# A scan and expert kernel whose engines' order is found by playing 2700 parts through, instead of by a table of places

## The chip, the cores and the metric

The kernel runs on one core of a Trainium2 chip. A core has several engines, each with its own queue of instructions that it works off in order: TensorE (PE in the profile; its weight loads are shown as PEld), VectorE (DVE), ScalarE (ACT), GpSimd (POOL) and SyncE (SP). SP and POOL issue the transfers between main memory and on-chip memory; POOL issues those whose rows are chosen by a list of indices. The engines run side by side and wait for each other through semaphores. Matrix products are written to PSUM, a small on-chip memory that is read by ACT and DVE.

The metric is the time on the device in microseconds (us), the median of three runs.

## The reference

The input x has 2 batches of 2048 tokens of 256 numbers, all in 32-bit floats. Each token is normalized (xn). Two branches are added to x:

```python
x = x + selective_scan_branch(xn) + moe(xn)
```

The scan branch puts each batch's tokens in the order of the cluster that they are nearest to (8 clusters, a stable sort), projects each sorted token to a step size and to two vectors B and C of 16 numbers, and then runs along the 2048 tokens, for each of 256 channels and 16 states:

```python
dA = jnp.exp(d_t[..., None] * A)
h = dA * h + (d_t * u_t)[..., None] * b_t[:, None, :]
y = jnp.einsum('bdn,bn->bd', h, c_t)
```

The result goes back to the tokens' first places. The expert branch picks for each token the two best of 8 experts and adds their outputs, weighted; an expert is `silu(x w1) * (x w3)`, 512 wide, times w2.

## The kernel before, in words

**The front** (until about 68 us) loads x, finds norms, clusters and experts, and writes the normalized rows to main memory (`xn`). It makes lists: which tokens the 71 expert tiles (128 rows each, of one expert) hold (`token_of`), which row of the weights each tile's loads start at (`w_row`), and which token stands at each place of the sorted order (`line_of`, by `list_rows`). The change does not touch the front.

**Expert tiles** (class `Tile`). Tile t goes through: `load_rows` gathers 128 rows (`xg_sb`, four buffers); `turn` transposes them on PE, copies them to `xT` on ACT and finds each row's share `own` on DVE; `up(0)` and `up(1)` are the products with w1 and w3 on PE, eight matmuls each, into one PSUM bank each; after `up(0)` comes a tanh on ACT, then `silu` on DVE, and after `up(1)` the `gate` on DVE; `down` is the product with w2 on PE, scaled on ACT (`yo`) and added to the sums in main memory (`acc`) by an indirect DMA of POOL. `load_up` and `load_down` fetch the weights for tile t + 3 into the buffers that tile t has left (1 MB and 0.5 MB). Where the expert is the same as three tiles before, the list of rows points outside and nothing is fetched. Every add into `acc` waits until the adds before it have landed (`wait_for_adds`).

**Scan pieces and steps** (classes `Piece` and `Step`). Each batch's sorted tokens are cut in four pieces of 512. A piece is gathered (`gather`, four indirect DMAs), transposed (`turn`), projected (`project`), its B and C are stored in main memory and loaded again spread over all partitions (`load_b`, `load_z`), and its step sizes are found (`step_size`, `decay_of_one`, `log`, `series`). A piece has four steps, by halves of states and of channels, which makes 32 steps. In a step ACT makes eight decays (`da`, `decay`), DVE makes four products `bu` (`feed`) and four scans over 1026 elements (`scan`), and PE turns the states (`turn`, 32 transposes into two PSUM buffers `pt_s`, copied to `ht` by ACT) and contracts them with C (`contract`, 32 matmuls into `y`). When a piece is done, `take_sums` copies its y and `add_sums` adds it to `acc` with four indirect DMAs. The last piece is added to the output itself, after `acc` has been copied there.

**What sets the order.** Each engine's queue holds its instructions in the order of the program's text; a chain of dependencies at the end of the kernel pins this. The text is written by hand. A list `lead` gives the first 13 expert jobs with the first piece's preparation between them. After that the steps are walked in eight places each: the even ones hold a scan, the odd ones a feed; places 1, 2, 4 and 5 turn the previous step's states in pairs, places 3 and 6 contract 16 matmuls at once. A table `plan`, filled by `at_place`, puts the next piece's preparation at fixed places. Expert jobs (`up(0)`, `up(1)`, and the previous tile's `down`, in this turn) are given out so that estimated PE work keeps a fixed ratio to estimated DVE work; `silu` and `gate` follow two places after their product (`later`).

## Time and profile before

| | us |
|---|---|
| median of 3 runs | 839.67 (839.21 to 841.74) |
| the profiled execution | 846.96 |
| its span, first to last instruction | 845.2 |
| PE, DVE, POOL, ACT busy | 728.7, 674.0, 577.3, 510.0 |
| first scan starts, last scan starts | 119.20, 821.65 |
| one scan, one feed on DVE | 2.297, 1.221 |
| last down-product of an expert tile ends | 801.5 |

A row of the profile names a line of the kernel, an engine, an operation, what is written and read (`out<-in`), how often, the busy time and the mean of one in ns, and the idle time before it with what ended it. In a listing in order of time the first two numbers are the start and the length in us. Matmuls of 32-bit floats show as two each. The spans on POOL are rough.

### The profile page before, as it was taken

How to read it: one execution, taken by the hardware profiler on the slowest of the kernel's cores; microseconds unless marked ns; L12 is line 12 of the kernel's file. 1: busy time of each engine (PE TensorE's matmuls, PEld its weight loads, DVE VectorE, ACT ScalarE, POOL GpSimd, SP SyncE). 2: the span in 40 equal slices, each digit the busy share in tenths (PEclk: the TensorE clock that was granted, in tenths of full speed). 3: DMA queues.
4: the chain of work that ended last, by engine and by line, in shares of the span. 5: the costliest groups of instructions: out<-in, count | busy, mean ns of one | idle time of the engine just before them, and what ended most of it. 6: DMA issues, size and time to landing. Idle time of an engine off the chain costs nothing.

```text
span 845.2 us, 16770 instructions
## 1 busy us (share of the span) xinstructions
PE 728.7 (86%) x6552; PEld 607.4 (72%) x6552; DVE 674.0 (80%) x849; ACT 510.0 (60%) x986; POOL 577.3 (68%) x374
## 2 busy tenths in 40 slices
PE   7376889789998998999989888899999898989564
PEld 5236677579987887788868776688778786979443
DVE  8964179589996989799879786788979897989590
ACT  4721265386667666866676565756695667757372
POOL 2024558677868778888868687886788888888412
PEclk9656999999999999999999999999999999999896
DMA  9683353854577548655674657556754855455472
GB/s 285 236 251 114 59 157 65 247 135 97 119 221 169 122 92 266 144 123 138 192 165 102 164 154 190 94 140 179 201 102 103 263 157 97 85 112 104 78 213 26
DMA packets 74015, 125.90 MB, mean 149 GB/s; under 512 B 24976, under 2 KB 42544, under 8 KB 70672
## 3 DMA queue, kind: packets, MB, share of 16 engines
q0 software_dynamic: 40224, 65.03, 32.7%
q1 hardware_dynamic: 33712, 59.80, 25.8%
q8 instruction: 52, 0.85, 0.4%
q14 instruction: 27, 0.22, 0.1%
HBM read 180.06 MB, written 27.00 MB: 245 GB/s over the span
## 4 chain that ended last, share of the span: by engine, by line
PE 51%; DMA 13%; ACT 11%; issue 9%; POOL 8%; DVE 7%; POOLq 0%; SPq 0%; ACTq 0%; DVEq 0%
PE p_ps L889 20%; PE py L912 10%; PE pt_s L800 7%; PE y L810 4%; POOL acc L830 4%; DMA w<-in_w_up_dram,w_row 4%; DMA w<-in_w_down_dram,w_row 4%; ACT ht L804 3%; POOL w L849 2%; ACT da L769 2%; DMA out_dram<-acc 2%; PE px L649 2%; PE pd L687 2%; PE pl L331 1%; DVE st L363 1%
## 5 line engine op out<-in xcount | busy, mean ns | idle before, releaser
L784 DVE TENSOR_TENSOR_SCAN hs<-da,bu 128x1026 f32<-128x1026 f32 x128 | 294.0, 2297 | 11.2 <-ACT da L769 1.9
L889 PE MATMUL p_ps<-xT,w 128*128 128x128 f32 x2272 | 280.2, 280 | 12.1 <-DMA w<-in_w_up_dram,w_row 5.3
L889 PEld LDWEIGHTS p_ps<-xT,w 128*128 128x128 f32 x2272 | 268.6, 195 | 29.0 <-issue 14.4
L830 POOL DMA_INDIRECT acc<-yo,token_of x71 | 141.0, 1985 | 68.8 <-ACT da L769 11.5
L769 ACT ACTIVATE da<-dl,na 128x512 f32<-128x512 f32 x256 | 181.3, 725 | 0.2 <-DVE hs L784 0.2
L912 PE MATMUL py<-w,g 128*128 128x256 f32 x568 | 145.8, 402 | 30.8 <-DMA w<-in_w_down_dram,w_row 19.2
L776 DVE TENSOR_TENSOR bu<-du,bt 128x1026 f32<-128x1026 f32 x128 | 156.3, 1221 | 19.5 <-ACT bt L756 15.7
L804 ACT COPY ht<-pt_s 128x512 f32<-128x512 f32 x256 | 137.3, 588 | 43.4 <-PE pt_s L800 36.7
L800 PE MATMUL pt_s<-ident,hs 128*128 128x128 f32 x1024 | 140.0, 280 | 20.0 <-ACT ht L804 14.6
L800 PEld LDWEIGHTS pt_s<-ident,hs 128*128 128x128 f32 x1024 | 115.7, 143 | 48.9 <-ACT ht L804 29.5
L849 POOL DMA_INDIRECT w<-in_w_up_dram,w_row x71 | 99.9, 1407 | 74.4 <-DVE w_row L578 36.2
L912 PEld LDWEIGHTS py<-w,g 128*128 128x128 f32 x568 | 107.4, 199 | 49.6 <-issue 14.2
L849 POOL DMA_INDIRECT w<-in_w_down_dram,w_row x71 | 111.7, 1573 | 21.6 <-issue 15.8
L863 POOL DMA_INDIRECT xg_sb<-xn,token_of x71 | 100.5, 1416 | 37.9 <-issue 17.4
L916 ACT ACTIVATE yo<-py,own 128x256 f32<-128x256 f32 x71 | 33.8, 476 | 103.9 <-PE py L912 99.1
L897 ACT ACTIVATE t_sb<-p_ps 128x512 f32<-128x512 f32 x71 | 42.5, 599 | 82.9 <-PE p_ps L889 71.5
L830 POOL DMA_INDIRECT acc<-yt,line_of x28 | 68.8, 2456 | 24.4 <-ACT ht L804 11.9
L902 DVE SCALAR_TENSOR_TENSOR t_sb<-t_sb,p_ps 128x512 f32<-128x512 f32 x71 | 48.5, 683 | 43.3 <-ACT t_sb L897 34.7
L810 PE MATMUL y<-ht,z 128*32 128x128 f32 x2048 | 76.8, 278 | 4.5 <-ACT ht L804 2.2
L810 PEld LDWEIGHTS y<-ht,z 128*32 128x32 f32 x2048 | 49.8, 109 | 25.3 <-ACT ht L804 11.3
L906 DVE SCALAR_TENSOR_TENSOR g<-t_sb,p_ps 128x512 f32<-128x512 f32 x71 | 48.4, 681 | 14.5 <-PE p_ps L889 8.9
L874 ACT COPY xT<-pt_g 128x256 f32<-128x256 f32 x71 | 26.8, 378 | 40.1 <-PE pt_g L872 40.0
(194 smaller groups left out, 580.0 us busy)
## 6 DMA issues: line engine op xcount, KB each, us to landing
bt<-bc SPq DMA_DIRECT2D x64, 512.0 KB
z<-bc SPq DMA_DIRECT2D x32, 256.0 KB
xn<-xt SPq DMA_DIRECT2D x8, 520.0 KB
xt<-in_x_dram SPq DMA_DIRECT2D x8, 512.0 KB
acc<-in_x_dram SPq DMA_DIRECT2D x8, 512.0 KB
w<-in_w_up_dram,w_row POOLq DMA_INDIRECT x71
w<-in_w_down_dram,w_row POOLq DMA_INDIRECT x71
xg_sb<-xn,token_of POOLq DMA_INDIRECT x71
```

The costliest lines, as they stand in the source:

```text
L769: nc.scalar.activation(self.da[o][:, n, 1:], self.piece.dl[:, self.h, :], AF.Exp, scale=na[:, self.h, state : state + 1],)
L776: nc.vector.tensor_mul(self.bu[o], self.piece.du[:, self.h, :].unsqueeze(1).to_broadcast([P, 2, CH1]), self.piece.bts[2 * self.s + o // 2] ...
L784: nc.vector.tensor_tensor_scan(self.hs.rearrange("p n t o -> p (n t) o")[:, :, o], self.da[o].rearrange("p n t -> p (n t)"), self.bu[o].re ...
L800: nc.tensor.transpose(pt[:, j, :], self.hs[:, n, t0 : t0 + G, :].rearrange("p t o -> p (t o)"), ident)
L804: nc.scalar.copy(self.ht[i], pt)
L810: nc.tensor.matmul(p.ys[self.h][j * G : (j + 1) * G, i, :], lhsT=p.zs[q][:, i * (P // G) + j, :], rhs=self.ht[i][:, j, :], start=False, st ...
L830: ins = nc.gpsimd.indirect_dma_start(out=to, out_offset=bass.IndirectOffsetOnAxis(ap=numbers, axis=0), in_=rows, in_offset=None, compute_o ...
L849: nc.gpsimd.indirect_dma_start(out=to[self.t % NW], out_offset=None, in_=rows, in_offset=bass.IndirectOffsetOnAxis(ap=w_row[:, self.t : se ...
L863: nc.gpsimd.indirect_dma_start(out=self.xg, out_offset=None, in_=xn_d, in_offset=bass.IndirectOffsetOnAxis(ap=token_of[:, self.t : self.t ...
L889: nc.tensor.matmul(p[:, f, :], lhsT=wk[:, h, f * P : (f + 1) * P], rhs=self.xT[:, h, :], start=h == 0, stop=h == ND - 1,)
L902: nc.vector.scalar_tensor_tensor(self.s, self.s, 1.0, self.p1, ALU.add, ALU.mult)
L912: nc.tensor.matmul(py, lhsT=self.g[:, f, :], rhs=w2[:, f, :], start=f == 0, stop=f == NH - 1)
```

## The change

The counts of scans, feeds, decays, matmuls and DMAs stay the same; what changes is where the order comes from. All steps above are cut into some 2700 parts, each on one engine: what was one method with a product, its copy by ACT and an add by POOL is now three (`turn`, `take_turned`, `find_own`; `up`, `tanh`; `down`, `take_down`, `add`). `contract` handles four matmuls at a time. The list of a batch's sorted rows (`list_rows`) becomes a class `RowList` with parts of its own, and its product with `part_p` moves from ACT to DVE.

A part has an engine, a cost in us, a due time, the parts that it needs, a time that its data take to land, and buffers that it takes until other parts have ended. `play` goes through the parts on paper: an engine that is free begins, among the parts that are able and whose buffers are free, the one with the smallest due time. The order in which parts begin is the order in which they are written to the text. The front, the tiles' buffers and the chain of dependencies at the end stay.

```diff
-    def list_rows(b: int, pos):
+    class RowList:
...
+            nc.vector.tensor_scalar(
+                self.num[:, 0], self.num[:, 2], part_p[:, self.b : self.b + 1], None, ALU.mult
+            )
...
-        def contract(self, n: int):
+        def contract(self, n: int, i: int):
             p, q = self.piece, 2 * self.s + n
-            for i in range(JC):
-                for j in range(P // G):
...
+            for j in range(P // G):
...
+    def play(parts, signal: float):
...
+        def able(p):
+            at = max([q.landed() + (signal if q.engine != p.engine else 0.0) for q in p.needs], default=0.0)
+            ready[p.engine].append((p.due, number[p], at, p))
...
+                r = min(able_now)
...
+                p.ended = busy[engine] = now + p.cost
+                begun.append(p)
...
+    slots = {
...
+            m=2, t=2, h0=1, h1=1, y0=1, y1=1, tok=4, member=1, xd=2, dl=2, du=2, w=1, b=2, z0=1, z1=1,
+            z2=1, z3=1, da=3, bu=2, hs=2, ht=4, yt=2, xT=2, own=6, s=2, g=2, yo=3, xg=4, add=1, lst=1,
...
+    END = 690.0
+    E0, S0 = 8.0, 45.0
+    TILE = (END - 30.0 - E0) / NT
+    STEP = (END - S0) / len(steps)
...
+        due = E0 + n * TILE
...
+            xg = Part(POOL, 1.25, due - 20.0, t.load_rows, (), 2.5)
+            wu = Part(POOL, 1.35, due - 20.0, t.load_up, [ups[n - NW]], 9.0)
+            wd = Part(POOL, 1.35, due - 18.0, t.load_down, [downs[n - NW]], 9.0)
+        turn = Part(PE, 0.3, due - 5.0, t.turn, [xg])
+        take = Part(ACT, 0.38, due - 8.0, t.take_turned, [turn])
+        own = Part(DVE, 0.4, due - 4.0, t.find_own, [xg])
+        up0 = Part(PE, 2.0, due, lambda t=t: t.up(0), [take, wu])
+        tanh = Part(ACT, 0.6, due - 8.0, t.tanh, [up0])
+        up1 = Part(PE, 2.0, due + 2.0, lambda t=t: t.up(1), [take, wu, up0])
+        silu = Part(DVE, 0.7, due - 8.0, t.silu, [tanh])
+        gate = Part(DVE, 0.7, due - 8.0, t.gate, [silu, up1])
+        down = Part(PE, 2.0, due + 4.0, t.down, [gate, wd])
+        yo = Part(ACT, 0.48, due - 2.0, t.take_down, [down, own])
+        add = Part(POOL, 1.95, due + 4.0, t.add, [yo], 2.5)
+        xg.take(slots["xg"], turn, own)
+        turn.take(slots["m"], take)
...
+                        Part(ACT, 0.73, at_o - 9.0, lambda st=st, i=i: st.decay(i), [series[2], *decay])
...
+                feed = Part(DVE, 1.25, at_o - 3.0, lambda st=st, o=o: st.feed(o), [series[3], begin_b])
+                scan = Part(DVE, 2.3, at_o, lambda st=st, o=o: st.scan(o), [feed, *decay, *step_scans[-1:]])
...
+                        PE, 0.55, at_i, lambda st=st, j=j, i=i: st.turn(j, i), [step_scans[-1], *step_turns[-1:]]
...
+                        PE, 0.15, at_i, lambda st=st, j=j, i=i: st.contract(j, i),
...
+            add = Part(POOL, 7.8, due + (SPP + 1) * STEP, lambda p=p: p.add_sums(acc_d), sums, 2.5)
...
+    for p in play(parts, 0.15):
+        p.do()
```

As built, PE's queue has each tile's `down` ahead of the next tile's second product, where before it stood behind both, and the transposes and contractions of a step stand in groups of four among the expert products. POOL's queue mostly has the down load of tile t + 3 ahead of tile t's add, where before it stood behind it. All expert tiles are through on PE before the transposes of step 30 (counted from 0), before the change ahead of those of step 29.

## The prediction

> **What bounds the kernel now.** I read the page first, then busy time by stretch, then the waits of TensorE (PE) inside the long stretch, then single rows. The page shows three engines near their limit and none at it:
>
> ```profile
> span 845.2 us, 16770 instructions
> ...
> PE 728.7 (86%) x6552; PEld 607.4 (72%) x6552; DVE 674.0 (80%) x849; ACT 510.0 (60%) x986; POOL 577.3 (68%) x374
> ```
>
> Busy time by stretch (columns: start and end, length, then PE, PEld, DVE, ACT, POOL, each with its count, granted clock, DMA share, GB/s):
>
> ```profile
> 68.00:120.00 52.00, 42.97 (x248) 34.80 (x249) 19.28 (x47) 20.13 (x34) 23.83 (x22) 0.84 0.45 126
> 120.00:790.00 670.00, 619.15 (x5813) 528.72 (x5811) 575.71 (x599) 436.30 (x853) 526.20 (x311) 0.99 0.60 145
> 790.00:801.50 11.50, 3.75 (x10) 2.96 (x11) 3.69 (x3) 0.49 (x2) 5.18 (x3) 0.70 0.28 37
> 801.50:845.00 43.50, 22.23 (x288) 15.90 (x286) 20.60 (x12) 21.88 (x42) 9.32 (x6) 0.81 0.46 116
> ```
>
> The stretches are: lead (first expert tiles until about the first scan), body, a hole, tail (no expert tiles left). In the body PE is busy 619.15 of 670 us (92%), VectorE (DVE) 86%. GpSimd (POOL) looks like 79%, but nearly every one of its 311 DMA instructions is preceded by about 0.30 us of idling, mostly put down to "issue": 526.2 + 311 x 0.30 = 619.5 us, also 92%. So PE idles only 50.9 us in the body, 9.0 in the lead and 7.75 in the hole: 67.6 us from 68 to 801.5, with 665.9 us of work. That idle time, and the tail's 43.7 us, are all that an order can win back. What PE waited for in the body (total, times, longest):
>
> ```profile
> PE py L912 <- DMA w<-in_w_down_dram,w_row: 10.8, 6, 3.8
> PE pt_s L800 <- ACT ht L804: 10.7, 14, 1.0
> PE py L912 <- ACT r L691: 6.0, 5, 2.0
> PE p_ps L889 <- DMA w<-in_w_up_dram,w_row: 5.3, 3, 2.7
> PE py L912 <- ACT u L636: 2.8, 5, 1.1
> PE p_ps L889 <- ACT xT L874: 2.7, 2, 1.5
> ...
> PE y L810 <- ACT ht L804: 2.2, 7, 0.5
> ```
>
> By kind: expert weights 16.1 us; turned states (ht) 12.9; other handovers with ScalarE (r, u, xT, yo, by all rows of that answer) 15.0; the remaining 6.9 small.
>
> **The change, part by part.** Counts of scans, feeds, matmuls and DMAs stay; the order of every queue is new from the first expert tile on.
>
> *Row lists.* For each of two lists the products by part_p go from ACT (0.396 us, L325) to DVE. No such DVE row exists; the nearest, L326 at 0.225 us, times 4 is 0.9 us, plus two small conversions of 0.17: 1.2 us of DVE, between 0 (the body has 94 us of idle DVE) and 1.2 if that cover goes. I take 0. The second list also no longer stands as one block in which DVE waits for PE: that was one wait of 8.2 us at 150 us, while PE itself waited 3.8 us for weights, so I count no separate gain.
>
> *Lead.* On PE the first turning of states now follows 7 tiles' up-products, not 9, but on DVE five gates, not four, stand before the first scan, and the four gathers of the first piece are mixed with weight loads that wait for tiles 0 and 1. One gate is 0.68 us; one tile on PE is 2 x 1.95 + 1.85 = 5.8 us. Between -6 and +6; I take 0 and keep 9.0 us idle.
>
> *Weights.* Still three buffers, so a load still waits for the tile three before. What moves is POOL's queue: before, every down load stood behind the same tile's add, which waits for the add before to land; now most stand ahead of it. The hole is such a case:
>
> ```profile
> 792.59 2.55 POOL L830 DMA_INDIRECT acc<-yo,token_of  x1 [7.44 <-DMA acc<-yt,line_of]
> 795.45 1.07 POOL L849 DMA_INDIRECT w<-in_w_down_dram,w_row  x1 [0.30 <-issue]
> ...
> 797.75 3.71 PE L912 MATMUL py<-w,g 128*128 128x256 f32 x8 [8.38 <-DMA w<-in_w_down_dram,w_row]
> ...
> 802.70 1.23 DVE L776 TENSOR_TENSOR bu<-du,bt 128x1026 f32<-128x1026 f32 x1 [8.90 <-ACT bt L756]
> ```
>
> The add waits 7.44 us, the load behind it goes out late, PE waits 8.38 us, ACT's yo behind PE, and DVE 8.90. In the new order the last down load follows the piece's four adds directly. So the hole's 7.75 us goes to 0, and down waits from 10.8 to 5 (between 0 and 10.8); up waits keep 5.3. That makes 10.3.
>
> *Handovers.* Copies out of PSUM are now parts of their own, and a PE part is written only when a PSUM slot is free on paper: ht 12.9 to 4.5, others 15.0 to 5. Ends: 0 and all 27.9; I lean to the low end because the durations written into the parts (scan 2.3, feed 1.25, decay 0.73, up 2.0) are those of the rows (2.297, 1.221, 0.725, 1.79 to 1.98). Small ones keep 6.9.
>
> *A new tightness.* Before, a whole other tile stood on PE between a tile's second up-product and its down-product: by row prices (up 1.94, eight transposes 1.04, sixteen contractions 1.08) a median 10.7 us. Now it is 2.2 us, and for 21 of 71 tiles 1.1 to 1.7. In that time DVE must do the gate, 0.68 us, behind whatever scan it has begun, 2.30. Queued behind a waiting down-product on PE are transposes and contractions, for which ACT and then DVE wait. Lower end 0; upper (2.30 + 0.68 - 2.2) x 71 = 55 us. I take, for the 21 tight ones, half a scan plus the gate less 1.4 us of cover: 0.43 x 21 = 9.0, nearer the low end, since the order was laid with these durations.
>
> *Finer grain.* Contractions stand in 196 runs instead of 64, transposes in 216 instead of 108. Each of 132 more contraction runs may cost nothing or the 0.17 us seen before contractions in the tail: 0 to 22; I take 0, since other matmuls follow at once in the body.
>
> *POOL.* The parts give it 5.9 us a tile (1.25 + 1.35 + 1.35 + 1.95); the rows say 1.42 + 1.41 + 1.57 + 1.99 + 4 x 0.30 = 7.6. It will run behind its paper times; whether PE feels that is a rival below. Its length comes from company on DVE (first minimum, median and maximum ns; then a load begun under a scan):
>
> ```profile
> L849 POOL DMA_INDIRECT w<-in_w_down_dram,w_row x71: 993/1415/3051, 44.1 to 795.5; - x71
> ```
>
> ```profile
> 119.20 2.30 DVE L784 TENSOR_TENSOR_SCAN hs<-da,bu 128x1026 f32<-128x1026 f32 x1
> 119.38 2.93 POOL L849 DMA_INDIRECT w<-in_w_up_dram,w_row  x1 [2.31 <-PE pt_g L872]
> ```
>
> The Trainium skill, page "SBUF — State Buffer", section "Who interferes with whom", says that a DVE instruction with two SBUF inputs contends with a GpSimd instruction that reads SBUF, and that the loser of the shared ports is blocked, not slowed. That speaks against a change that packs DVE more tightly. Taken strictly, scans and feeds would shut POOL out for 294 + 156 us, and with 396 us at its shortest durations and 103 of issue it would need 949 us, more than this span; the rows above, which reach 3 us but have a median of 1.4, disagree, and the sum goes by them.
>
> *Tail.* Behind the last gate stood eight scans, now five; behind the last down-product 96 transposes and 96 contractions, now 76 and 84. Two paths lead to the last adds:
>
> ```profile
> 811.12 1.21 SPq L1141 DMA_DIRECT2D out_dram<-acc  x2
> ...
> 824.09 3.79 PE L800 MATMUL pt_s<-ident,hs 128*128 128x128 f32 x16 [4.88 <-DVE hs L784]
> ...
> 833.79 1.54 POOL L830 DMA_INDIRECT out_dram<-yt,line_of  x1 [24.93 <-ACT yt L731]
> ```
>
> Scans: last gate, 5 x 3.52 = 17.6, then 9.6 as from 823.95 to 833.5, less 3.7 until the last down-product: 23.5 us after it. Copy: 801.5 to 826.4 was 25.0 (chain of waits: 811.74 plus 14.70); up to 30 if a fourth add must land first. I take 25.0, then 11.4 for the last adds as now (833.8 to 845.2): 36.5 instead of 43.7, between 35 and 41.4. The 20 transposes and 12 contractions add 3.4 us to PE's work before that, and the last down-product, 3.71 us at clock 0.70, gives back 1.9.
>
> **Sum.** Idle: 9.0 + 10.3 + 9.5 + 6.9 + 9.0 = 44.7. Span: 68 + 665.9 + 1.5 + 44.7 + 36.5 = 816.6 (before by the same sum: 68 + 665.9 + 67.6 + 43.7 = 845.2). The profiled run took 846.96, 1.8 over its span and 7.3 over the median 839.67, so the median is 816.6 + 1.8 - 7.3 = 811.
>
> **Rivals.**
> - *The paper order holds fully.* Only the lead's 9.0 us stay idle and the tail is 35: 68 + 667.4 + 9 + 35 = 779, median 774 to 795 with some rest. For it: durations on PE, DVE and ACT match the rows. Against: POOL does not, and weights still come three tiles ahead.
> - *Lockstep (the other side).* PE and DVE wait for each other at nearly every tile because the 2.2 us of cover are less than a scan plus a gate (2.98): 55 in place of 9.0 gives a span of 863, median 857. It decides from 28.6 us more idle than my sum, 0.40 us a tile. For it: the 21 tight tiles and POOL's drift. Against: the paper has DVE free at that moment.
> - *POOL sets the pace.* Its work from 64.3: 564.5 + 344 x 0.30 less the last four adds, 660 us. With DVE denser (86 to 93%) busy time grows 8%, 45 us; if it also keeps its 51 us of body waits, then with 30.5 from landing to end the span is 851, median 845. Half of these waits: 819. Against: loads now stand ahead of adds.
> - *No use.* Idle time only changes place: 67 us of it with the shorter tail, median 833.
>
> **How the numbers follow.** Likeliest (795 to 832) 0.42; paper order 0.18; POOL or idle moved, split: 832 to 837 0.05, within 0.3% (837.2 to 842.2, about what three runs of 839.21 to 841.74 can tell) 0.04, POOL above that 0.13; lockstep 0.18. Faster 0.65, same 0.04, slower 0.31. The range is 776 to 868: below lies little of the paper case, above the worse half of lockstep with finer grain. The likeliest alone: 795 to 832.
>
> **What would show it.** Right: the 8.4 us wait of py for down weights gone; PE waits on r, u and xT below 5 us; PE idle in the body under 45 us; fewer than six scans behind the last gate; the last adds released by the copy, not by yt. Wrong: PE rows waiting on DVE g, or DVE's t_sb waiting on ACT, each well over 10 us; POOL busy plus issue above 97% with PE waiting for w or xg_sb; granted clock falling below 0.97 in the body, which would raise the price of every matmul.

## The result, and the profile after

The changed kernel takes 880.39 us (median of 4 runs, 879.78 to 885.34) against 840.70 for the kernel before on the same chip: a ratio of 1.047 (95% interval 1.042 to 1.053). It is slower. The forecast of 811 us had the wrong sign, and its range (776 to 868) does not hold the time.

The page of the kernel after, its span and its busy times:

```profile
span 878.5 us, 16650 instructions
...
PE 761.4 (87%) x6552; PEld 608.3 (69%) x6552; DVE 674.1 (77%) x853; ACT 520.1 (59%) x982; POOL 545.8 (62%) x374
```

The profiled execution took 880.27 us. The one of the kernel before took 846.96, 6.3 over the median of its four runs, so its idle time in particular is rather too high for a comparison. PE's idle time over the whole span is 878.5 - 761.4 = 117.1 us, about as before (116.5). What grew is PE's busy time: 761.4 instead of 728.7, for the same 6552 matmul passes. DVE's busy time is the same to 0.1 us.

Busy time by stretch (columns as in the prediction: start and end, length, then PE, PEld, DVE, ACT and POOL with their counts, granted clock, DMA share, GB/s). The first scan starts at 122.82, the last down-product ends at 842.9:

```profile
68.00:120.00 52.00, 42.81 (x273) 36.31 (x274) 23.55 (x72) 17.14 (x29) 33.18 (x32) 0.86 0.54 144
120.00:830.00 710.00, 646.61 (x5738) 524.27 (x5736) 570.26 (x582) 448.66 (x854) 486.80 (x302) 0.95 0.54 136
830.00:842.90 12.90, 12.13 (x113) 10.04 (x114) 12.47 (x9) 8.25 (x17) 4.88 (x3) 1.00 0.28 32
842.90:878.50 35.60, 19.50 (x244) 12.41 (x241) 13.99 (x9) 14.83 (x26) 8.32 (x5) 0.84 0.52 137
```

These rows give the terms of the prediction's sum. Work of PE from 68 us to the last down-product: 42.81 + 646.61 + 12.13 = 701.6 us, where 667.4 were forecast. Idle time there: 9.2 in the lead and 64.2 behind it, 73.4, where 44.7 were forecast. Tail: 35.6, forecast 36.5. So of the 61.9 us by which the span misses the forecast, 34.2 are work and 28.7 are idle time, less 0.9 of the tail. The body's clock is 0.95, not 0.99.

What PE waited for between 120 and 830 us (total, times, longest):

```profile
PE py L970 <- DVE g L964: 19.0, 6, 7.6
PE py L970 <- issue: 16.3, 3, 8.4
PE p_ps L945 <- DVE t_sb L960: 6.5, 2, 4.0
PE y L862 <- ACT ht L856: 6.1, 2, 5.4
PE pl L535 <- DVE num L526: 4.2, 1, 4.2
...
PE pt_s L850 <- ACT ht L856: 2.9, 5, 1.3
```

The waits for weights are gone, and so are those for r, u and xT. In their place PE waits for `g`, the gate of DVE, in a few waits of many microseconds. DVE itself waits for something that it hardly waited for in the kernel before (first the row before, then the row after):

```profile
DVE own L876 <- DMA xg_sb<-xn,token_of: 2.1, 2, 1.4
```

```profile
DVE own L932 <- DMA xg_sb<-xn,token_of: 87.4, 24, 9.3
```

That is `find_own`: two short instructions that read a tile's gathered rows. The change made them a part of their own that needs only the rows, and the play on paper can write them as soon as the rows have landed there. In the chip's queue everything of DVE behind them then waits for the rows too. The listing in time of the kernel after shows five such waits and the down-product that each ends in:

```profile
325.00 0.22 DVE L932 SCALAR_TENSOR_TENSOR own<-xg_sb,te 128x1 f32<-128x1 f32 x1 [4.94 <-ACT ht L856]
...
329.05 3.78 PE L970 MATMUL py<-w,g 128*128 128x256 f32 x8 [3.93 <-DVE g L964]
...
461.92 0.99 POOL L915 DMA_INDIRECT xg_sb<-xn,token_of  x1 [0.30 <-issue]
...
468.19 0.22 DVE L932 SCALAR_TENSOR_TENSOR own<-xg_sb,te 128x1 f32<-128x1 f32 x1 [9.29 <-DMA xg_sb<-xn,token_of]
...
473.54 0.68 DVE L960 SCALAR_TENSOR_TENSOR t_sb<-t_sb,p_ps 128x512 f32<-128x512 f32 x1
474.33 0.69 DVE L964 SCALAR_TENSOR_TENSOR g<-t_sb,p_ps 128x512 f32<-128x512 f32 x1
...
475.07 3.47 PE L970 MATMUL py<-w,g 128*128 128x256 f32 x8 [7.64 <-DVE g L964]
...
557.38 0.22 DVE L932 SCALAR_TENSOR_TENSOR own<-xg_sb,te 128x1 f32<-128x1 f32 x1 [6.37 <-DMA xg_sb<-xn,token_of]
...
564.28 3.75 PE L970 MATMUL py<-w,g 128*128 128x256 f32 x8 [6.45 <-issue]
...
660.16 0.22 DVE L932 SCALAR_TENSOR_TENSOR own<-xg_sb,te 128x1 f32<-128x1 f32 x1 [6.43 <-DMA xg_sb<-xn,token_of]
...
664.36 3.75 PE L970 MATMUL py<-w,g 128*128 128x256 f32 x8 [8.43 <-issue]
...
693.98 0.22 DVE L932 SCALAR_TENSOR_TENSOR own<-xg_sb,te 128x1 f32<-128x1 f32 x1 [8.21 <-DMA xg_sb<-xn,token_of]
...
698.03 3.78 PE L970 MATMUL py<-w,g 128*128 128x256 f32 x8 [5.84 <-DVE g L964]
...
831.10 1.89 PE L970 MATMUL py<-w,g 128*128 128x256 f32 x8
```

Follow the one at 468: POOL issues the gather at 461.92, DVE has stood at `own` since 458.90 and gets the rows at 468.19. Work that the paper put next, then `silu` (t_sb) and the gate, end at 475.0, and PE, which ran out of work at 467.4, starts the down-product then. The product takes 3.47 us; a down-product that follows other matmuls takes 1.89, as the last line shows. The five idle times are 32.3 us together, nearly all of the 35.3 us that PE waited at `py`. The rows named "issue" belong to the same kind: there too DVE's gate ended just before (564.18, 664.26). The wait of `own` that ended at 325.00 is put down to `ht`, but by the trace's semaphore records that tile's rows had landed only 0.06 us before `ht`, so this one is a wait for rows too.

On some chips a single run of the kernel before was near 824.5 us, some 15 below the median; the ratio compares the fastest group of runs only and then stands up to 1.3% above the quotient of the medians, so both are given, and a step on which they differ is called so.

The end is as forecast but for one detail: five scans stand behind the last gate, but the last adds are still released by `yt` (21.1 us of POOL's waiting), not by the copy. So the tail's forecast came out by another path than the one it was worked out from.

### The profile page after: what moved, and what is told of

It is laid out like the page before. It is cut to its first block, busy times and chain, and to the rows that moved or that the text cites. A ratio compares the mean times of both kernels' runs of the same rounds, so it can differ in the third digit from the quotient of the medians.

```text
span 878.5 us, 16650 instructions
## 1 busy us (share of the span) xinstructions
PE 761.4 (87%) x6552; PEld 608.3 (69%) x6552; DVE 674.1 (77%) x853; ACT 520.1 (59%) x982; POOL 545.8 (62%) x374
## 5 line engine op out<-in xcount | busy, mean ns | idle before, releaser
L945 PEld LDWEIGHTS p_ps<-xT,w 128*128 128x128 f32 x2272 | 270.4, 195 | 24.9 <-issue 12.4
L970 PE MATMUL py<-w,g 128*128 128x256 f32 x568 | 154.1, 419 | 40.7 <-issue 21.5
L882 POOL DMA_INDIRECT acc<-yo,token_of x71 | 150.4, 2119 | 62.4 <-ACT da L818 13.7
L856 ACT COPY ht<-pt_s 128x512 f32<-128x512 f32 x256 | 146.9, 587 | 69.2 <-PE pt_s L850 67.7
L850 PE MATMUL pt_s<-ident,hs 128*128 128x128 f32 x1024 | 160.1, 285 | 9.3 <-DVE hs L833 4.7
L970 PEld LDWEIGHTS py<-w,g 128*128 128x128 f32 x568 | 113.7, 211 | 61.9 <-issue 25.1
L901 POOL DMA_INDIRECT w<-in_w_down_dram,w_row x71 | 98.8, 1392 | 79.9 <-PE py L970 64.4
L850 PEld LDWEIGHTS pt_s<-ident,hs 128*128 128x128 f32 x1024 | 114.0, 143 | 42.6 <-issue 30.8
L915 POOL DMA_INDIRECT xg_sb<-xn,token_of x71 | 92.8, 1308 | 40.1 <-issue 30.8
L862 PE MATMUL y<-ht,z 128*32 128x128 f32 x2048 | 98.7, 286 | 6.4 <-ACT ht L856 6.4
L932 DVE SCALAR_TENSOR_TENSOR own<-xg_sb,te 128x1 f32<-128x1 f32 x71 | 15.3, 216 | 92.4 <-DMA xg_sb<-xn,token_of 87.4
L882 POOL DMA_INDIRECT acc<-yt,line_of x28 | 62.3, 2224 | 34.8 <-issue 8.6
L862 PEld LDWEIGHTS y<-ht,z 128*32 128x32 f32 x2048 | 44.4, 109 | 55.2 <-issue 30.7
```

The lines of the kernel that those rows point to most:

```text
L850: nc.tensor.transpose(self.pt[:, j, :], self.hs[:, n, t0 : t0 + G, :].rearrange("p t o -> p (t o)"), ident)
L856: nc.scalar.copy(ht, self.pts.pop((n, i)))
L862: nc.tensor.matmul(p.ys[self.h][j * G : (j + 1) * G, i, :], lhsT=p.zs[q][:, i * (P // G) + j, :], rhs=ht[:, j, :], start=False, stop=q == ...
L882: ins = nc.gpsimd.indirect_dma_start(out=to, out_offset=bass.IndirectOffsetOnAxis(ap=numbers, axis=0), in_=rows, in_offset=None, compute_o ...
L901: nc.gpsimd.indirect_dma_start(out=to[self.t % NW], out_offset=None, in_=rows, in_offset=bass.IndirectOffsetOnAxis(ap=w_row[:, self.t : se ...
L915: nc.gpsimd.indirect_dma_start(out=self.xg, out_offset=None, in_=xn_d, in_offset=bass.IndirectOffsetOnAxis(ap=token_of[:, self.t : self.t ...
```

## The experiments

Four theories were tested. *Row theory* (A in the expectations): DVE's early wait for late rows makes gates late. *Lockstep* (B): too little cover between second up-product and down-product. *POOL* (C): the paper gives POOL's work less time than it takes. *Short runs* (D): the cost of more and shorter runs of matmuls on PE. Each run is compared with the kernel before on its own chip; a step that an edit "gives back" is the difference of two entries of the third column. Every edit of the paper has the whole order found anew, on every engine, and no run changed the order by an edit that should not matter, to show what that alone does; a step of some 10 us is therefore not surely the price of the number that was edited. PE idle is span less busy time. "Behind own" is the idle time of PE, in waits over 1 us from 120 us on, before up- and down-products that began within 9 us of the end of a wait of DVE at `own` of over 1 us, summed from the listings in time. Busy and idle times are those of the profiled execution; for three kernels it was far from the median: before (846.96), f3 (835.5) and i3 (829.5, the fastest of its four).

| kernel | us, median | against before's median, same chip | ratio (95%) | PE busy | PE idle | DVE wait at own | behind own |
|---|---|---|---|---|---|---|---|
| after | 880.4 | +39.7 | 1.047 (1.042, 1.053) | 761.4 | 117.1 | 87.4 | 39.0 |
| e1 own late | 869.9 | +31.9 | 1.034 (1.027, 1.041) | 754.7 | 116.6 | none | 0 |
| e2 rows land 8 | 853.2 | +15.2 | 1.015 (1.010, 1.020) | 752.5 | 99.3 | 45.7 | 24.9 |
| e3 POOL costs | 860.3 | +22.3 | 1.025 (1.020, 1.029) | 753.1 | 108.9 | 63.0 | 32.6 |
| e4 gate cover | 869.4 | +31.4 | 1.037 (1.031, 1.043) | 758.5 | 106.7 | 75.9 | 33.9 |
| f1 contract 16 | 880.0 | +40.5 | 1.059 (1.043, 1.074) | 732.1 | 147.0 | 91.5 | 59.5 |
| f2 and turns in eights | 866.4 | +26.9 | 1.044 (1.031, 1.057) | 731.6 | 130.5 | 86.7 | 36.0 |
| f4 f2 and rows land 8 | 844.2 | +4.7 | 1.018 (1.004, 1.034) | 720.7 | 119.9 | 60.2 | 32.3 |
| h1 down behind add | 887.3 | +47.5 | 1.070 (1.053, 1.086) | 763.4 | 121.2 | 97.7 | 44.4 |
| i1 handover 1.0 | 873.3 | +34.9 | 1.053 (1.037, 1.070) | 753.8 | 115.2 | 85.5 | 32.6 |
| j1 POOL regular | 899.5 | +54.7 | 1.053 (1.043, 1.064) | 775.7 | 125.1 | 106.4 | 30.8 |
| h2 e1 and e2 | 861.1 | +21.3 | 1.033 (1.010, 1.057) | 755.0 | 108.7 | none | 0 |
| h3 f4, own late, six buffers | 851.7 | +11.8 | 1.021 (0.989, 1.053) | 720.0 | 131.6 | none | 0 |
| i3 f4 and POOL costs | 845.9 | +7.5 | no verdict | 719.4 | 108.3 | 54.2 | 28.4 |
| k1 i3, rows land 14 | 850.7 | +10.6 | 1.010 (1.004, 1.016) | 727.3 | 122.2 | 59.4 | 19.7 |
| *kernel before* | | | | 728.7 | 116.5 | 2.1 | 0 |
| f3 before, short runs | 842.4 | +2.9 | 1.014 (1.002, 1.027) | 742.0 | 91.7 | none | 0 |
| h4 before, own early | 838.4 | -1.4 | 1.007 (1.002, 1.012) | 727.9 | 108.2 | 33.3 | 8.4 |
| i4 before, down early | 841.1 | +2.7 | 1.013 (0.995, 1.030) | 731.5 | 109.2 | none | 0 |
| i5 before, all four | 843.1 | +4.7 | 1.016 (1.001, 1.031) | 748.6 | 92.9 | 4.2 | 0 |

### One number of the paper at a time

**e1.** find_own also needs the tile's silu, so DVE is no longer asked for it early.

```diff
         silu = Part(DVE, 0.7, due - 8.0, t.silu, [tanh])
+        own.needs.append(silu)
```

> In the changed kernel DVE waits 87 us, 24 times, at the part find_own for gathered rows (xg_sb), with scans and gates queued behind it. Here find_own needs its tile's silu besides, so that the rows must be in use before DVE comes to it; nothing else is edited (the order is found anew). Theory A (DVE's early wait for rows makes the slowdown): the 87 us fall below 10, PE's waits for the gate (19 us) fall with them, and the time falls from 880 to 825 to 850. Theory B (too little cover between gate and down-product): the waits move to gate and tanh, time 865 to 885. Theory C (POOL behind its paper times): PE now waits for the same rows at pt_g, 20 to 60 us of it, time 855 to 880.

The wait at `own` is gone, and only 8 of the 39.7 us come back, far from the row theory's 825 to 850. Taking `find_own` out of DVE's way is thus not a cure. The rows are still late; now PE meets them, and late weights as well, as the POOL theory had it (waits of PE in e1):

```profile
PE pt_g L923 <- DMA xg_sb<-xn,token_of: 24.7, 4, 12.3
PE p_ps L945 <- DMA w<-in_w_up_dram,w_row: 15.7, 6, 8.0
PE p_ps L945 <- DVE t_sb L960: 13.2, 3, 8.1
```

**e2.** The rows take 8.0 us to land on paper. The profile's 2.8 to 6.6 us with a median of 3.8, which the expectation names, covers only the 8 of 71 gathers of the kernel after whose landing it could tell; in the 18 waits of over 1 us that it puts down to them or to `ht` behind 120 us, `own` started 3.6 to 11.2 us after its gather, in the median 6.9.

```diff
-            xg = Part(POOL, 1.25, due - 20.0, t.load_rows, (), 2.5)
+            xg = Part(POOL, 1.25, due - 20.0, t.load_rows, (), 8.0)
```

> The landing time of a tile's gathered rows is 8.0 us on paper instead of 2.5 (the profile shows 2.8 to 6.6, median 3.8, from issue to landing); both the transposes and find_own are planned later by it. Theory A: the wait at find_own falls from 87 us to 20 to 40 and the time to 845 to 865. Theory B: no change, 870 to 885. Theory C: the rows are late because POOL issues them late, not because they land late, so the wait falls only by a third and the time stays at 860 to 880.

This is the largest single step, 24.5 us, clear by the ratios too (1.015 against 1.047) and in the row theory's range, though the wait fell less than it said. The median time from a gather's start to its `own`, over all 71 tiles of the traces, goes from 9.1 to 14.4 us (14.8 in the kernel before).

**e3.** POOL's costs as the rows of before measure them, with the 0.30 us that POOL idles ahead of each transfer.

```diff
-            xg = Part(POOL, 1.25, due - 20.0, t.load_rows, (), 2.5)
-            wu = Part(POOL, 1.35, due - 20.0, t.load_up, [ups[n - NW]], 9.0)
-            wd = Part(POOL, 1.35, due - 18.0, t.load_down, [downs[n - NW]], 9.0)
+            xg = Part(POOL, 1.72, due - 20.0, t.load_rows, (), 2.5)
+            wu = Part(POOL, 1.71, due - 20.0, t.load_up, [ups[n - NW]], 9.0)
+            wd = Part(POOL, 1.87, due - 18.0, t.load_down, [downs[n - NW]], 9.0)
...
-        add = Part(POOL, 1.95, due + 4.0, t.add, [yo], 2.5)
+        add = Part(POOL, 2.29, due + 4.0, t.add, [yo], 2.5)
```

The gathers of a piece go from 1.3 to 1.67, its four adds from 7.8 to 11.0.

> POOL's paper costs are those of the rows with 0.30 us of issue (gather of rows 1.72, up load 1.71, down load 1.87, add 2.29, piece gather 1.67, piece add 11.0, instead of 1.25, 1.35, 1.35, 1.95, 1.3, 7.8). Theory C: the plan and the chip agree on POOL, DVE's wait at find_own falls below 30 us and the time to 820 to 850. Theory A: the wait falls less, to 40 to 70 us, because rows still land late behind weights, time 855 to 875. Theory B: no change, 870 to 885.

17 us come back, clear by the ratios too: POOL's paper times matter, and with them the wait at `own` is shorter, though not below 30 us.

**e4.** The gate counts as done 2.0 us later on paper, so that the down-product is written later.

```diff
-        gate = Part(DVE, 0.7, due - 8.0, t.gate, [silu, up1])
+        gate = Part(DVE, 0.7, due - 8.0, t.gate, [silu, up1], 2.0)
```

> The gate lands 2.0 us later on paper, so that a down-product is planned at least 2 us after its gate on DVE. Theory B: PE's waits for the gate (19 us on PE) fall below 5 and the time falls by 15 to 30 us, to 850 to 865. Theories A and C: the waits for rows at find_own stay above 70 us and the time stays within 10 us of 880.

PE's wait for `g` is gone; 22.4 us of waiting for `t_sb`, the silu on the same queue of DVE, have taken its place, and of the time only 8 us come back. The idle time behind `own` is 33.9 us instead of 39.0: cover at the gate alone moves the wait to another product.

### Short runs

**f1** handles sixteen contractions as one part (cost 1.0 in place of four times 0.15, which is also nearer to what they take); **f2** also the transposes in eights; **f4** is f2 with rows landing after 8.0 us.

```diff
-                    contract = Part(
-                        PE, 0.15, at_i, lambda st=st, j=j, i=i: st.contract(j, i),
-                        [take, masks[q], begins[st.h]],
-                    )
...
+                contract = Part(
+                    PE, 1.0, at_i, lambda st=st, j=j: [st.contract(j, i) for i in range(JC)],
+                    [*taken, masks[q], begins[st.h]],
+                )
```

f2 besides:

```diff
-                        PE, 0.55, at_i, lambda st=st, j=j, i=i: st.turn(j, i), [step_scans[-1], *step_turns[-1:]]
+                        PE, 0.95, at_i, lambda st=st, j=j, i=i: [st.turn(j, i), st.turn(j, i + 1)],
+                        [step_scans[-1], *step_turns[-1:]],
```

> The changed kernel with 16 contractions in one part, as before the change (64 runs of contractions on PE instead of 196); transposes stay in fours. Theory D (a short run costs PE a fixed extra): by rows of the changed kernel whose next run starts without a wait, 8 passes take 0.36 us from start to start, 16 take 0.58, 32 take 1.01, so a run costs 0.143 us besides 0.0272 a pass; 132 runs fewer are 18.9 us, so PE's busy time falls from 761 to 738 to 745 and the time from 880 to 855 to 865. Theory A (only the early wait for rows counts): PE's busy time may fall, but the time stays at 870 to 885.

> As the run with 16 contractions, and the state transposes in pairs of eight as well (122 runs on PE instead of 216). Theory D: 8 transposes at a time take 0.93 us from start to start, two fours 0.98, and breaks in the up-products fall too: 10 us more, PE busy 728 to 738, time 842 to 856. Theory A: 865 to 885.

> Coarse contractions and transposes together with rows that land 8.0 us after issue on paper. If the early wait for rows (27 us by the run with that landing time) and the short runs (theory D, 29 us) are separate and both real, the time is 822 to 832, below the kernel before. If they are the same loss seen twice, 843 to 853.

PE's busy time falls by 29 us in f1 and the time not at all, against the 855 to 865 us of the theory of short runs: the gain goes into idle time, above all these two rows (waits of PE in f1):

```profile
PE py L970 <- DVE g L964: 41.8, 18, 12.4
PE p_ps L945 <- DVE t_sb L960: 25.4, 6, 7.5
```

f2 gives 13 us by the medians, but by the ratios (1.044 against 1.047) nothing clear of noise. f4, with rows landing later, gives another 22 and stands 4.7 us over the kernel before. By the medians that is 10 us better than e2 alone (15.2), by the ratios no better (1.018 and 1.015), and 844.2 lies in the range that the expectation gave for one loss seen twice. Whether the longer runs gain time on top of the later rows is open.

**f3.** The other way round: in the kernel before, the first half's contractions and the second half's transposes of each step stand in alternating fours (160 runs of contractions instead of 64).

```diff
-            elif i in (1, 2, 4, 5):
+            elif i in (1, 2):
...
-                    before_.turn(i // 4, (i - 1) % 3 * 2 + j)
-            elif i in (3, 6):
-                before_.contract(i // 4)
+                    before_.turn(0, (i - 1) * 2 + j)
+            elif i in (4, 5):
+                for j in range(2):
+                    m = (i - 4) * 2 + j
+                    before_.contract(0, [m])
+                    before_.turn(1, m)
+            elif i == 6:
+                before_.contract(1, range(JC))
```

> The kernel before, with one part of the change alone: the first half's 16 contractions of a step are split in fours and mixed with the second half's transposes (160 runs of contractions instead of 64, 175 of transposes instead of 108). Theory D: 96 x 0.143 + 67 x 0.05 to 0.1 = 17 to 20 us of PE, which is 92% busy, so the time rises from 838 to 850 to 860 and PE's busy time from 729 to 742 to 750. Theory A: within 5 us of 838.

PE's busy time rises by 13.3 us, and the median is 3 us over the kernel before (12 by the ratio). Idle time is 24.8 us less, but up to 14 of that may lie in the choice of executions (846.96 us for the kernel before, 835.5 for f3). Short runs do cost PE work; how much of it is paid in time lies between 3 and 12 us.

### The suspected properties in the regular order of before

**h4.** find_own of tile t + 1 stands where that of tile t stood; from gather to `own` it is 7.1 us in the median instead of 14.8.

```diff
         tiles[t].turn()
+        if t == 0:
+            tiles[0].find_own()
+        if t + 1 < NT:
+            tiles[t + 1].find_own()
```

> The kernel before, with the two DVE instructions that find a tile's share moved one tile ahead (about 9 us), all else in its place: the suspected part alone. Row theory: of the 14.7 us between a row gather's issue and its own some 6 are left, DVE waits for rows in 25 to 90 us in all (2.1 now), gates come late, and the kernel is 1 to 3% slower (848 to 865 us). Rival: a DVE wait for rows is harmless, since DVE has 94 us of idle time in the body; then own waits as much but the time stays within 0.5% of 839 us.

```profile
DVE own L879 <- DMA xg_sb<-xn,token_of: 33.3, 16, 5.4
```

DVE waits 33.3 us for rows, and the median is 1.4 us below that of before (the ratio says 0.7% above). So the wait by itself costs between nothing and 6 us: the 8.4 us of PE's idle time behind it stand before up-products, none before a down-product. The row theory's 1 to 3% slower did not come; the rival held, if not to the letter.

**i4.** Each down-product between the next tile's up-products, as in the changed order. **i5.** That, find_own early, the short runs of f3, and the down load ahead of the tile's add on POOL.

```diff
         if t < NT:
-            jobs += [part_up(t, 0), part_up(t, 1)]
+            jobs.append(part_up(t, 0))
         if t > 0:
             jobs.append(part_down(t - 1))
+        if t < NT:
+            jobs.append(part_up(t, 1))
```

> The kernel before, with each tile's down-product set between the two up-products of the next tile in place of behind both: the tightness of the changed order alone. If the missing cover costs by itself, PE waits for g in 10 to 30 us in all (none before) and the time rises by 5 to 20 us, 845 to 860 us. Rival: one up-product (1.94 us) and what stands beside it cover a gate as well, and the time stays within 0.5% of the kernel before.

> The kernel before with four properties of the changed order put in by hand: down-products early, find_own one tile ahead, contractions and half of the transposes in fours, down loads ahead of the tile's add on POOL. If these properties make the loss, they add up to most of the 40 us: 865 to 885 us, own's wait over 60 us, POOL's down load waiting for PE in over 40 us. Rival: in a regular order none of them costs, and the loss is in the irregular order that the paper play writes (rows in bursts, scans in pairs); then 838 to 850 us.

Neither loses more than 5 us by the medians, or 13 by the ratio. In i4 the gate is never late for a product by more than 0.8 us: PE waits for `g` 1.6 us in all, not 10 to 30. But i5 is not the full sum of its parts: its wait at `own` is only 4.2 us, so long waits together with little cover were not reproduced in the order of before. What i5 does price is short runs, early down-products and POOL's down load at the head of its queue (35.9 us of waiting there, 64.4 in the kernel after): small, in a regular order.

### Cures in the paper that did not help

**h1** puts the down load behind the add of the tile three before, as it stood; **i1** gives every handover between engines 1.0 us; **j1** ties POOL's transfers of expert tiles into the fixed round of the kernel before.

```diff
-            wd = Part(POOL, 1.35, due - 18.0, t.load_down, [downs[n - NW]], 9.0)
+            wd = Part(POOL, 1.35, due - 18.0, t.load_down, [downs[n - NW], adds[n - NW]], 9.0)
```

```diff
-    for p in play(parts, 0.15):
+    for p in play(parts, 1.0):
```

```diff
+            if n > NW:
+                wu.go_behind(last_down)
+                xg.go_behind(last_up)
+                adds[n - 1 - NW].go_behind(xg)
+            wd.go_behind(adds[n - NW])
+            last_up, last_down = wu, wd
```

(`go_behind` is a need that counts from the end of the other part's issue, not its landing.)

> The kernel after, but a tile's down load may be written only after the add of the tile three before (the place it had before the change). Queue theory: the 64 us in which POOL's down load stands at the head of its queue and waits for PE's down-product hold up the row gathers behind it; with the load behind the add this wait falls below 15 us, DVE's wait for rows at own from 87 us to 40 or less, and the time from 880 to 850 to 862 us. Rival, row slack: the rows are late because paper gives them 2.5 us to land and POOL runs behind its paper times; then own keeps 60 us or more and the time stays within 870 to 885 us.

> The kernel after, with every handover between engines taken as 1.0 us on paper in place of 0.15; nothing else. Theory of a tight paper (no place on PE, DVE or ACT has slack against a POOL that runs behind its paper times, so that every lateness is passed on): slack everywhere gives at least 25 us, 840 to 855 us, and DVE's wait for rows falls from 87 to below 60 us although the landing time of rows stays. Row theory (only the 2.5 us for rows to land are wrong): at most 10 us, 870 to 885 us, own's wait stays over 75 us.

> The kernel after, with POOL's expert transfers tied on paper into the fixed round of the kernel before (rows of the next tile, add of the tile three before, its down load, the next up load), each behind the one before it; costs, due times and all other engines' rules as in the kernel after. Theory of an irregular order on POOL (rows in bursts of three, then none for 20 us, adds two at a time): the lead of rows in the trace becomes even, own's wait falls from 87 to below 40 us, and the time from 880 to 840 to 855 us. Rival, the irregular order on DVE and PE (two scans or three finds in a row before a gate, short runs): own's wait may fall but the time stays in 865 to 885 us.

None moves the wait at `own` below 85 us; by the medians i1 gives back 5 us, h1 and j1 lose another 8 and 15. The idea behind h1 was that POOL's down load, waiting at the head of its queue for PE's down-product, makes the rows behind it late. h1 does not test that, and neither does j1: the wait only goes from the down load to the add, which needs `yo` and so the same down-product (waits of POOL, first after, then h1, then j1):

```profile
POOL w L901 <- PE py L970: 64.4, 22, 7.5
POOL acc L882 <- ACT yo L976: 10.7, 6, 3.0
```

```profile
POOL acc L882 <- ACT yo L976: 53.1, 18, 11.1
```

```profile
POOL acc L882 <- ACT yo L976: 76.3, 23, 8.6
```

All waits of POOL over 0.4 us, from 120 us to the last down-product and added from the traces, are 154 us in the kernel after, 157 in h1 and 154 in j1; they are 61 in the kernel before, 120 in e2 and 98 in f4. In e1 the two rows above are down to 8.7 and 6.8 us and the kernel is still 32 us slower than before, so they are not the whole loss; whether POOL's waiting for PE makes the rows late is left open. j1 does speak against bursts: its gathers are evenly spaced (the shortest tenth of the intervals ends at 7.2 us, 1.7 in the kernel after and 6.7 in the kernel before), and the wait at `own` is longer, 106.4 us. What i1 says agrees with the row theory: a microsecond everywhere does not help against rows that come 4 to 9 us late.

### Everything together

**h2** is e1 and e2; **h3** is f4 with e1's edit and six row buffers; **i3** is f4 with e3's costs; **k1** is i3 with rows landing after 14.0.

```diff
-            self.xg = ffn.tile([P, D + SH], F32, tag="xg", name="xg_sb", bufs=4)
+            self.xg = ffn.tile([P, D + SH], F32, tag="xg", name="xg_sb", bufs=6)
```

> The kernel after with both halves of the row cause taken: rows land after 8.0 us on paper, and find_own needs the tile's silu; the short runs of contractions and transposes stay. Row theory: landing alone gave 27 us and own later alone 10.5 us; if both remove the same wait, the time is 848 to 856 us with own under 10 us. If the waits are separate the gains add up to 842 us. Rival, fine grain: PE busy stays near 752 us and the rest of the loss, 10 to 15 us over the kernel before, stays; only if the time reaches 840 or less is the fine grain free.

h2 came out as neither side had it: DVE's wait at `own` is gone, and the kernel is no faster than e2 alone (21.3 us over the kernel before against 15.2; 1.033 against 1.015, with overlapping intervals). PE now waits 30.6 us for the rows at `pt_g`, as in e1. This points to the late rows as what costs, whichever engine meets them, and not to `own` alone.

> The kernel after with transposes in eights, contractions in sixteens, rows landing after 8.0 us on paper, find_own after silu, and six row buffers in place of four (the rows may be asked for two tiles earlier). Row theory: without own's wait (60 us in the run with landing and coarse parts) and with rows early enough that PE does not wait for them, PE busy 721 us plus some 100 us of idling as now gives 820 to 835 us, faster than both kernels. Rival: the idle time is set by the order of POOL and DVE as a whole and moves to other waits (PE on t_sb, weights); then 838 to 848 us.

> The kernel with coarse transposes and contractions and rows landing after 8.0 us on paper, and POOL's costs on paper as the rows measure them (1.67 to 2.29 us in place of 1.25 to 1.95, four adds 11.0). Theory of POOL behind its paper times: the three corrections, worth 14, 27 and 20 us alone, add up in part; own's wait falls from 60 to below 30 us, PE idle from 120 to 105 us, and the time is 825 to 838 us, at or below the kernel before. Rival, idle time moves: own's wait falls but PE waits for weights or t_sb in its place; 840 to 850 us.

> The kernel with coarse transposes and contractions and POOL's measured costs on paper, and rows landing after 14.0 us on paper in place of 8.0; four row buffers as in both kernels. Theory of late rows (own's wait of 54 us is what is left of the loss): own's wait falls below 20 us and the time by another 8 to 20 us, to 826 to 838 us, below the kernel before. Rival, the idle time moves on: own's wait falls, but waits on t_sb, up weights or hs grow by as much, as in the run with six buffers, and the time stays within 1% of the kernel with 8.0 us, 838 to 854 us.

With six buffers and no wait at `own`, the rows are early (45.9 us from gather to `own` in the median), but PE waits for weights instead (waits of PE in h3). A tile's gather starts 30.7 us before its up load in h3, 20.9 in f4 (medians); that the earlier gathers delay the weights fits this and is not shown:

```profile
PE p_ps L945 <- DMA w<-in_w_up_dram,w_row: 30.9, 9, 8.9
```

i3 has the median 845.9 (829.5 to 854.9) against 838.4 (824.4 to 844.8): by the medians 32 of the 39.7 us are back, but its runs spread over 25 us and do not settle the comparison, and the kernel before is not beaten. k1 asked whether DVE's remaining wait still costs. The wait did not fall:

```profile
DVE own L932 <- DMA xg_sb<-xn,token_of: 59.4, 13, 14.9
```

So k1 leaves that question open: there are still 19.7 us of PE idling behind `own`, and 28.4 in i3, and no run took them away without a new wait of the same size.

## Why the prediction was wrong

**The sum's first term, PE's work.** The prediction took "665.9 us of work" as given and *Finer grain* at 0 between 0 and 22 us. The work measured 34.2 more. The listing shows why (kernel after; contractions of 8 and of 16 passes, each followed by the next run):

```profile
840.50 0.43 PE L862 MATMUL y<-ht,z 128*32 128x128 f32 x8
840.86 1.99 PE L970 MATMUL py<-w,g 128*128 128x256 f32 x8
842.78 0.64 PE L862 MATMUL y<-ht,z 128*32 128x128 f32 x16
843.35 1.09 PE L850 MATMUL pt_s<-ident,hs 128*128 128x128 f32 x8
```

From start to start a run of 8 passes takes 0.36 us and one of 16 takes 0.57; 24 and 32 passes, elsewhere, 0.79 and 1.01. That is 0.14 us for the run and 0.027 for each pass. 132 more runs make 19 us. For transposes (0.49 for 4, 0.93 for 8) it is 0.05 a run, 5 us for 108 more. The five down-products above, 3.5 to 3.8 us instead of 1.89, add 9.1. Together 33 us, an estimate that agrees with the 34.2, but not part by part. Counted in the trace from each pass's start to the next one's, contractions took 13.0 us more than before, transposes 5.1, down-products 11.3 and up-products 5.9, all else 2.6 less: the 64 long contraction runs of the kernel before were dearer (72.5 us) than those of f1 (66.6). f1 takes 18.9 us off the contractions, as the estimate has it, and 10 more off other products, so most of the work does hang on the grain. The argument for 0, "other matmuls follow at once", was wrong: 0.14 us a run, near the 0.17 seen in the tail, holds in the body too. Its price in time is another matter: none in f1, 13 us by the medians and nothing clear of noise by the ratios in f2, 3 to 12 in the order of before for two thirds as many extra runs (f3).

**The missing term, late rows.** This is the step that failed in time. The sum took 22.9 us of idle time away; instead it grew by 5.8. The prediction listed `find_own` as a new part and never asked what stands behind it on DVE. Under *POOL* it said that POOL "will run behind its paper times" and left "whether PE feels that" to a rival about POOL's throughput. POOL's throughput did not bind: busy plus issue is 486.80 + 302 x 0.30 = 577 of 710 us, 81%, and not over 97%. PE felt it through DVE: the paper had the rows after 2.5 us, in the waits above 1 us they came 6.9 us after the gather's start in the median, and 87.4 us of waiting fall on the queue that also holds silu and gate; 39.0 us of PE's idling stand behind it. Later rows on paper (e2) give 24.5 us back and POOL's measured costs (e3) 17. Moving `find_own` alone (e1, h2) does not: then PE itself waits for the rows.

**Lockstep.** The prediction asked how long a gate is behind a scan (0.43 us in each of 21 tight tiles, 9.0 in all) and expected many small waits. There are few and long ones, 35.3 us at `py` in the body, behind `own`. A wait of 5 to 9 us at `own` is longer than the cover of 2.2 us; the wait alone (h4: 33.3 us, with a shorter median from gather to own, 7.1 us, than the kernel after, 9.1) and the small cover alone (i4) each cost little in the order of before. That the pair is what costs is argued from the trace of after and these two runs, not shown; the pair alone was not reproduced (i5).

**Right.** *Weights*: the hole and the 8.4 us wait are gone, and all weight waits with them, more than the 10.3 us counted. *Handovers*: r, u and xT gone, and ht at 9.0 us where 4.5 were forecast. *Lead*: 9.2 us of idle time, 9.0 forecast, but mostly by two waits of 5.2 us, at `pl` (in part before 68 us) and at `py`, that the prediction did not have: luck. *Tail*: 35.6 against 36.5, by scans and `yt` and not by the copy: luck in part. *Row lists*, costed at 0, show as one wait of 4.2 us in the body (pl for num) and one of 5.2 in the lead (1.4 in each before). The gains at weights and handovers are real, and PE's idle time from 68 us to the last down-product is still 73.4 us because the new waits are larger.

**The strict lock.** By the Trainium skill, page "SBUF — State Buffer", section "Who interferes with whom", read strictly, a span of 949 us was worked out; the trace again disagrees: DVE's busy time is unchanged (674.1), POOL's fell from 577.3 to 545.8, and the span is 878.5. The section speaks of a GpSimd instruction that reads SBUF, "not with one that only writes it"; that the issue of an indirect DMA is such a read was the prediction's own assumption, and no run here shows it. The granted clock of 0.95 in the body, which the prediction named as a sign against it, goes with a longer mean matmul (a contraction 286 ns, 278 before).

**What stays open.** Runs e2 and e3 show that much of the loss comes back when the paper's numbers for rows and POOL are put right; that longer runs add to it (f2, f4, and i3 with 32 of 39.7 us) stands on medians alone. They do not show why the rows are late, whether by POOL's waiting for PE or by its load, nor which order on POOL would serve rows and weights at once. Nor is it settled why i3, with 54.2 us of DVE waiting for rows, is within 1% of the kernel before by the medians; removing that wait without delaying the weights was not achieved.

## What to carry to other kernels

When an order is found by a play on paper, look for each part that waits for a transfer on an engine that also holds others' critical work: a needed time of landing that is short by a few microseconds becomes a wait of everything queued behind it, so put in the measured landing and issue times before anything else (24 and 17 us here; a wider margin of 14 us, k1, did not help). Take a landing time from the waits that it ends and not only from a profile's median. What a wait in an in-order queue costs depends on what stands behind it: 33 us of waiting cost at most 6 us where a down-product had some 10 us of cover (h4). When an edit takes one wait away, look whether the same cause makes another, as in h1. And count the runs on PE when work is cut finer: equal passes are not equal time.

## What was not expected of the hardware

A contraction run costs about 0.14 us besides its passes, so that the same 2048 passes, from start to next start, took 85.5 us in the kernel after and 66.6 in f1 with 132 runs fewer. A down-product that follows 4 to 8 us of idling of PE ran 3.5 to 3.8 us instead of 1.89. And 29 us less work on the busiest engine, at 87% of the span, gained no time (f1: 880.0 us, ratio 1.059 against 1.047).
